# Another order of the seven products of an LSTM gate, other additions, and other places for the work beside them

## The chip, the cores and the metric

One core of a Trainium2 chip runs the whole program: TensorE (matrix products), VectorE, ScalarE and GpSimd (additions, activations), SyncE (which here issues transfers). The metric is the time on the device, in microseconds (us), from the first to the last instruction of one execution. Nothing is computed on the host except the layout of the inputs.

## What is computed

The reference is a stack of four residual layers on x (128 batches, 64 tokens, 256 channels) in float32; each is `x = x + layer(relu(layernorm(x)))`. Layers 0, 2 and 3 (a graph network with batch norm, and two kinds of attention) are not touched by the change. Layer 1 is:

```python
h = relu(einsum('ts,bsh->bth', adj, x @ Wg0 + bg0))      # "convolution"
h = relu(einsum('ts,bsh->bth', adj, h @ Wg1 + bg1))
for p in range(1, MAX_SKIP + 1):                         # p = 1, 2, 3, 4
    nw = T // p                                          # windows of p tokens
    wins = h[:, :nw * p, :].reshape(B * nw, p, H)
    last = lstm_last(Wih[p-1], Whh[p-1], bih[p-1], bhh[p-1], wins)
    h = h.at[:, arange(nw) * p + (p - 1), :].set(last)   # the last token of each window
# one LSTM step; gates i, f, g, o
g = x_t @ Wih.T + h @ Whh.T + bias
c = sigmoid(f) * c + sigmoid(i) * tanh(gg)
h = sigmoid(o) * tanh(c)
```

## The kernel before

The tokens go through layer 1 in eight superchunks of 1,024. A superchunk runs the LSTMs of p = 1 (`single`), 2, 3 and 4 (`lstm`) one after the other, each with p steps. Beside them, at the places where the generator of the LSTMs yields, stand pieces of other work: the two convolutions of the next superchunk (`convolutions`), the residual sums of the last one, and the start of layer 2 (`ahead`).

A 256 x 256 product of a gate is made of seven 128 x 128 products instead of eight, with sums of operands made beforehand (`operands_x` on GpSimd for x, `differences` on VectorE for h). A `Unit` is one gate at one step. Each of its products has an x part and an h part, added up by TensorE in a PSUM bank. Products 1, 6, 7 and 4 of a unit use one "x" bank one after the other, so each must be read before the next is written; product 5 uses a "y" bank, 2 and 3 the halves of a "z" bank. There are two banks of each letter.

```python
class Unit:                                   # cut
        self.of = {1: "x", 6: "x", 7: "x", 4: "x", 5: "y", 2: "z", 3: "z"}
    def copy(self, kind):                     # ScalarE: product 1 or 5 out of its bank
        nc.scalar.copy(gate(self.q, kind // 5, halves[kind // 5]), self.psum(kind))
    def add(self, dst, a, kind):              # VectorE: gate = gate + bank
        nc.vector.tensor_add(gate(self.q, *dst), gate(self.q, *a), self.psum(kind))
    def c11(self): self.add((0, halves[0]), (0, halves[0]), 2)
    def u4(self):  self.add((0, halves[1]), (1, halves[1]), 6)    # reads product 5's copy
    def c12(self): self.add((0, halves[1]), (0, halves[1]), 3)
    def c22(self): self.add((1, halves[1]), (1, halves[1]), 7)
    def act(self, part): ...                  # ScalarE; act(2) reads product 4 in the bank

for s in range(1, p):                         # one step; pe(k) = product k, do(f) = other engines
    last = s == p - 1
    B = [Unit(q, s) for q in (1, 3)]          # A: gates 0 and 2 (i, g); B: gates 1 and 3 (f, o)
    ...
    each(A, pe(5, "h"), do("copy", 5), pe(1), do("copy", 1), pe(3, "h"), pe(6, "x"), pe(6, "h"),
         pe(2, "h"), do("u4"), do("c11"), do("c12"))
    each(B, pe(5), do("copy", 5))
    each(A, do("act", 0), pe(7), do("c22"), do("act", 1))
    each(B[:1], pe(3), pe(2))
    each(A, pe(4), do("act", 2))
    nc.gpsimd.tensor_mul(gates[:, 0, :, :n], gates[:, 0, :, :n], gates[:, 2, :, :n])
    each(B[1:], pe(3), pe(2))
    each(B, pe(1), do("copy", 1))
    yield                                     # the middle of a step: an even place
    each(B, pe(6))
    A = [] if last else [Unit(q, s + 1) for q in (0, 2)]
    each(A, pe(5, "x"))
    def cell(c, part): ...                    # two VectorE operations, then tanh on ScalarE
    if last:
        ...                                   # see the diff
    else:
        for u in B:
            each([u], do("u4"), do("c11"), do("c12"), do("act", 0))
        cell(0, every)
        each(B, pe(7), do("c22"))
    each(B, do("act", 1))
    each(A[:1], pe(3, "x"), pe(2, "x"))
    new_state(s, 0, every)                    # VectorE; h for the next step, channels 0 to 127
    if not last: dh[0]()
    each(A[1:], pe(3, "x"), pe(2, "x"))
    each(B, pe(4))
    B[0].act(2); cell(1, halves[1]); B[1].act(2); cell(1, halves[0])
    new_state(s, 1, halves[1]); ...; new_state(s, 1, halves[0]); ...; dh[2]()
    yield                                     # the end of a step: an odd place
```

`each(us, f, g)` does f for every unit of `us`, then g. The places of a superchunk are numbered: 0 to 3 lie in `single`; 4, 8 and 14 between the first and the second half of the first products of p = 2, 3 and 4; 5, 9 and 15 ahead of their first step; then an even number for the middle and an odd one for the end of each step (6, 7; 10 to 13; 16 to 21). `CONV`, `BEGUN`, `FIRST` (the first superchunk) and so on say at which place each piece of the other work is put.

The engines' instructions stand in the order in which the program names them[...].

Of the kernel before, what the change touches and what calls it, by code (L numbers as in the profile page):

```python
# [19 lines left out]
def kernel(  # L20
# [23 lines left out]
    B, T, D = x.shape  # L44
# [12 lines left out]
    SUP = 2  # L57
# [531 lines left out]
    with tc.manual_schedule(engines={mybir.EngineType.PE, mybir.EngineType.DVE,  # L589
# [27 lines left out]
        for c in range(2, NCH - 1):  # L617
            a, z = sevens[c], sevens.get(c - 1)
# [273 lines left out]
    hTs = {}  # L892
# [87 lines left out]
    def convolutions(c):  # L980

        y, h = conv_tile(c)
        for m in range(KD):
            scaled(y, c, m)

        mid = res.tile([P, Q, CH * KD // Q], F32, tag=f"r{c}", name=f"ym_{c}")
        for k in range(KD):
            nc.vector.transpose(
                mid.rearrange("p b (j k c) -> p k j b c", j=NJ, k=KD)[:, k],
                y[:, k, :].rearrange("p (j b t) -> p j b t", b=Q, t=32))  # L990
        far = put(mid, f"y{c}")
        dst = y.rearrange("p k (q n) -> p (k q) n", q=2)
        get(dst, far)
        xs[c] = res.tile([P, NJ, D], F32, tag=f"r{c}", name=f"xs_{c}")
        nc.sync.dma_start(xs[c], xr[c])
        yield
        add_squares(xs[c], xs[c], dst)
        yield
        stats = ln_stats(xs[c], f"b{c}")
        yield  # L1000
        yield from apply_halves(h, xs[c], stats, f"b{c}")
        banks = aggregate(h, adjt_bd, f"b{c}")
        yield
        for e, ps in enumerate(banks):
            nc.vector.tensor_copy(by_batch(y)[:, e], ps)
        yield
        banks = product_v(c, y)
        yield
        bounded(y, banks)
        yield  # L1010
        banks = product_u(c, y)
        yield
        biased(h, banks)
        yield
        banks = aggregate(h, adjt_bd, f"c{c}")
        yield
        for e, ps in enumerate(banks):
            to_hT(c, e, ps)
            yield
# [30 lines left out]
    def lstm(p, hv, name, follows, x1, ending):  # L1050
# [3 lines left out]
        n = nb * nw  # L1054
# [85 lines left out]
        class Unit:  # L1140
# [25 lines left out]
            def c11(self):  # L1166
                self.add((0, halves[0]), (0, halves[0]), 2)

            def u4(self):
                self.add((0, halves[1]), (1, halves[1]), 6)  # L1170

            def c12(self):
                self.add((0, halves[1]), (0, halves[1]), 3)

            def c22(self):
                self.add((1, halves[1]), (1, halves[1]), 7)
# [9 lines left out]
        def each(us, *fs):  # L1186
            for f in fs:
                for u in us:
                    f(u)

        def pe(kind, parts="xh"):
            return lambda u: u.product(kind, parts)

        def do(f, *a):
            return lambda u: getattr(u, f)(*a)
# [4 lines left out]
        for s in range(1, p):  # L1200
            last = s == p - 1
            B = [Unit(q, s) for q in (1, 3)]
            if not last:
                ox[s + 1] = operands_x(p, hv, name, s + 1)
            each(A, pe(5, "h"), do("copy", 5), pe(1), do("copy", 1), pe(3, "h"), pe(6, "x"), pe(6, "h"),
                 pe(2, "h"), do("u4"), do("c11"), do("c12"))
            each(B, pe(5), do("copy", 5))
            each(A, do("act", 0), pe(7), do("c22"), do("act", 1))
            each(B[:1], pe(3), pe(2))
            each(A, pe(4), do("act", 2))  # L1210
            if last:
                load_sets(2)
            nc.gpsimd.tensor_mul(gates[:, 0, :, :n], gates[:, 0, :, :n], gates[:, 2, :, :n])  # L1213
            each(B[1:], pe(3), pe(2))
            each(B, pe(1), do("copy", 1))
            yield
            each(B, pe(6))
            A = [] if last else [Unit(q, s + 1) for q in (0, 2)]
            each(A, pe(5, "x"))

            def cell(c, part):
                nc.vector.tensor_mul(cells[:, c, part], cells[:, c, part], gate(1, c, part))
                nc.vector.tensor_add(cells[:, c, part], cells[:, c, part], gate(0, c, part))  # L1223
                nc.scalar.activation(gate(2, c, part), cells[:, c, part], AF.Tanh)  # L1224

            if last:

                each(B[:1], do("u4"), do("c11"), pe(7))
                each(B[1:], do("u4"), pe(7))
                each(B[:1], do("c22"), do("c12"), do("act", 0))  # L1230
                each(B[1:], do("c22"), do("c11"), do("c12"), do("act", 0))
                cell(0, every)
            else:
                for u in B:
                    each([u], do("u4"), do("c11"), do("c12"), do("act", 0))
                cell(0, every)
                each(B, pe(7), do("c22"))
            each(B, do("act", 1))
            each(A[:1], pe(3, "x"), pe(2, "x"))
            new_state(s, 0, every)  # L1240
            if not last:
                dh[0]()
            each(A[1:], pe(3, "x"), pe(2, "x"))
            each(B, pe(4))
            B[0].act(2)
            cell(1, halves[1])
            B[1].act(2)
            cell(1, halves[0])
            new_state(s, 1, halves[1])
            if not last:  # L1250
                dh[1]()
            new_state(s, 1, halves[0], nc.gpsimd if follows and last else nc.vector)
            if last:
                load_sets(2)
                ending()
            else:
                dh[2]()
            yield
# [212 lines left out]

    RESIDUAL = (0, 3, 4), (2, 5, 6)
    CONV = (3, 4, 4, 5, 6, 7, 8, 9, 10, 10), (3, 4, 4, 11, 12, 13, 14, 15, 16, 17, 18, 20)
    BEGUN = (11, 13, 14, 16), (17, 19)
    BEGUN_FIRST = (12, 15, 16, 18), (19, 21)
    FIRST = (1, 3, 3, 4, 4, 5, 6, 7, 8, 9, 10, 11, 12, 12), (3, 6, 7, 8, 10, 13, 14, 15, 16, 17, 18, 19, 20, 20)
    AHEAD = (4, 5, 7, 12, 14, 15), (6, 7)
    LATE = 5, 6, 8, 9  # L1480
    IDLE = {5: 4, 7: 18, 9: 10, 13: 14, 15: 8}
    FINAL = (4, 5, 10, 12, 12, 14), (6, 7, 11, 14, 14, 16)
    START = (0, 1, 0, 0, 0, 1, 0, 1, 1, 0, 0, 1, 1, 0, 1)

    tc.no_sync_barrier()
    with tc.manual_schedule(engines={mybir.EngineType.PE, mybir.EngineType.DVE, mybir.EngineType.Pool,
# [21 lines left out]
    with tc.manual_schedule(engines={mybir.EngineType.PE, mybir.EngineType.DVE, mybir.EngineType.Pool,  # L1508
                                     mybir.EngineType.Activation, mybir.EngineType.SP}):
        last = NCH // SUP - 1  # L1510
        for sc in range(last + 1):
            todo = {}

            def units(places, unit):
                for n in places:
                    todo.setdefault(n, []).append(unit)
# [17 lines left out]
                    units((FINAL if sc == last else AHEAD)[i], aheads[(sc - 1) * SUP + i])  # L1534
            if sc + 1 < last:
                for i in range(SUP):
                    units((BEGUN if sc else BEGUN_FIRST)[i], convs[(sc + 2) * SUP + i])
            for n, _ in enumerate(lstms(sc, hTs[sc])):
                for u in todo.pop(n, ()):
                    next(u)  # L1540
                if sc == last and n in IDLE:
                    keep_busy(IDLE[n], f"l{n}")
                if sc == last and n == 8:

                    new_hT(sc + 1)
                    for c in range(SUP):
                        load2(c, hTs[sc + 1][:, c, :].rearrange("p (q n) -> p q n", q=Q))
# [530 lines left out]
```

## Time and profile before

| | |
|---|---|
| device time, median of 3 runs | 1891.58 us (1890.7 to 1891.86) |
| span of the profiled execution | 1890.8 us |
| TensorE matmul, weight load, busy share | 99%, 78% |
| VectorE, ScalarE, GpSimd, busy share | 65%, 54%, 29% |
| first superchunk of layer 1 (274.2 to 437.1 us) | 162.9 us |
| each of the next five, which are alike | 155.6 us |
| seventh | 155.9 us |
| eighth, to its last LSTM product | 145.5 us |

The ends of matmuls are modelled in this profile, so "busy" holds short waits too; starts are recorded, and the distance from one start to the next shows them. Each float32 product of the program is two instructions of TensorE in the trace. In groups, "x<-xd" says which tile is written and which is read: x, y, z are the banks above, xd and hd the sums of operands of x and of h, hs and hT the states and the tokens themselves.

### The profile page before, as it was taken

How to read it: one execution, taken by the hardware profiler on the slowest of the kernel's cores; microseconds unless marked ns; L12 is line 12 of the kernel's file. 1: busy time of each engine (PE TensorE's matmuls, PEld its weight loads, DVE VectorE, ACT ScalarE, POOL GpSimd, SP SyncE). 2: the span in 40 equal slices, each digit the busy share in tenths (PEclk: the TensorE clock that was granted, in tenths of full speed). 3: DMA queues.
4: the chain of work that ended last, by engine and by line, in shares of the span. 5: the costliest groups of instructions: out<-in, count | busy, mean ns of one | idle time of the engine just before them, and what ended most of it. 6: DMA issues, size and time to landing. Idle time of an engine off the chain costs nothing.

```text
span 1890.8 us, 39088 instructions
## 1 busy us (share of the span) xinstructions
PE 1863.0 (99%) x15077; PEld 1479.3 (78%) x15077; DVE 1236.6 (65%) x3150; ACT 1016.6 (54%) x2284; POOL 551.4 (29%) x704
## 2 busy tenths in 40 slices
PE   8999989999999999999999999999999999999998
PEld 6877856886897798699589689878969967777776
DVE  6768845567476666667667666665565567676776
ACT  5766544456456446555655645655565544444453
POOL 5856622122222212212322321222122114332232
PEclk9999999999999999999999999999999999999999
DMA  3224643135333433332433343343144254444433
GB/s 114 73 66 150 234 175 105 49 116 184 106 129 139 151 129 129 110 124 114 151 118 139 141 151 129 129 135 117 52 135 154 71 157 135 143 148 142 139 113 113
DMA packets 111273, 241.45 MB, mean 128 GB/s; under 512 B 11504, under 2 KB 74864, under 8 KB 111088
## 3 DMA queue, kind: packets, MB, share of 16 engines
q1 hardware_dynamic: 110192, 237.09, 37.4%
q8 instruction: 119, 1.95, 0.4%
q0 software_dynamic: 320, 1.05, 0.2%
q10 hardware_dynamic: 576, 0.82, 0.1%
q14 instruction: 66, 0.54, 0.1%
HBM read 170.50 MB, written 68.42 MB: 126 GB/s over the span
## 4 chain that ended last, share of the span: by engine, by line
PE 90%; DVE 5%; ACT 2%; issue 1%; POOL 1%; DMA 1%; SPq 0%; DVEq 0%; ACTq 0%
PE x L1155 23%; PE z L1155 11%; PE g L1126 9%; PE y L1155 6%; PE v L1568 6%; PE x L1329 4%; PE y L1329 3%; PE u L929 3%; PE p_q L1575 3%; PE v L915 3%; PE X L1764 3%; PE X L423 2%; PE X L499 2%; PE Y L1764 1%; PE Y L423 1%
## 5 line engine op out<-in xcount | busy, mean ns | idle before, releaser
L1164 DVE TENSOR_TENSOR gates<-gates,x 128x128 f32<-128x128 f32 (+2 forms) x384 | 118.5, 321 | 326.3 <-PE x L1155 319.1
L1155 PE MATMUL x<-xd,wset 128*128 128x128 f32 (+2 forms) x1152 | 256.8, 311 | 0.7 <-DVE gates L1164 0.2
L1155 PE MATMUL x<-hd,wset 128*128 128x128 f32 (+2 forms) x1152 | 246.7, 303 | 0.0
L1213 POOL TENSOR_TENSOR gates<-gates 128x512 f32<-128x512 f32 (+2 forms) x48 | 75.0, 1562 | 551.8 <-ACT gates L1084 551.8
L1084 ACT ACTIVATE gates<-gates,bias 128x256 f32<-128x256 f32 (+4 forms) x384 | 170.3, 490 | 56.2 <-DVE gates L1164 52.7
L1155 PEld LDWEIGHTS x<-xd,wset 128*128 128x128 f32 x1152 | 180.8, 190 | 19.0 <-DVE gates L1164 6.1
L1155 PEld LDWEIGHTS x<-hd,wset 128*128 128x128 f32 x1152 | 185.1, 191 | 5.0
L1126 PE MATMUL g<-hT,wset 128*128 128x256 f32 (+2 forms) x576 | 183.9, 474 | 1.1 <-DVE hT L1095 1.1
L1126 PEld LDWEIGHTS g<-hT,wset 128*128 128x128 f32 x576 | 108.6, 190 | 69.8 <-issue 38.5
L1161 ACT COPY gates<-y 128x128 f32<-128x128 f32 (+2 forms) x192 | 54.3, 294 | 202.3 <-PE y L1155 201.8
L1155 PE MATMUL z<-hs,wset 128*128 128x128 f32 (+2 forms) x768 | 154.0, 303 | 0.0
L1155 PE MATMUL z<-hT,wset 128*128 128x128 f32 (+2 forms) x768 | 148.4, 306 | 0.0
L1155 PEld LDWEIGHTS z<-hs,wset 128*128 128x128 f32 x768 | 119.8, 191 | 3.3
L1155 PEld LDWEIGHTS z<-hT,wset 128*128 128x128 f32 x768 | 117.9, 192 | 4.4 <-ACT gates L1113 0.5
L1161 ACT COPY gates<-x 128x128 f32<-128x128 f32 (+2 forms) x192 | 56.6, 296 | 93.5 <-PE x L1155 92.8
L1164 DVE TENSOR_TENSOR gates<-gates,z 128x128 f32<-128x128 f32 (+2 forms) x384 | 104.5, 316 | 0.1
L1084 ACT ACTIVATE gates<-x,bias 128x128 f32<-128x128 f32 (+2 forms) x192 | 74.8, 390 | 49.3 <-PE x L1155 46.5
L1113 ACT ACTIVATE gates<-g,bias 128x512 f32<-128x512 f32 (+2 forms) x144 | 74.6, 560 | 30.7 <-PE g L1126 30.2
L1155 PE MATMUL x<-hT,wset 128*128 128x128 f32 (+2 forms) x384 | 85.7, 305 | 0.4 <-ACT gates L1084 0.2
L1155 PE MATMUL x<-hs,wset 128*128 128x128 f32 (+2 forms) x384 | 84.9, 303 | 0.0
L1224 ACT ACTIVATE gates<-cell 128x256 f32<-128x256 f32 (+2 forms) x144 | 55.3, 384 | 51.9 <-DVE cell L1223 50.3
L1155 PE MATMUL y<-xd,wset 128*128 128x128 f32 (+2 forms) x384 | 77.4, 304 | 3.9 <-ACT gates L1113 3.3
(326 smaller groups left out, 4144.6 us busy)
## 6 DMA issues: line engine op xcount, KB each, us to landing
wset<-wfar SPq DMA_DIRECT2D x96, 960.0 KB, 6.5
hT<-far_h SPq DMA_DIRECT2D x124, 128.0 KB, 3.1
far_h<-hm SPq DMA_DIRECT2D x16, 512.0 KB, 2.8
far_n<-xs SPq DMA_DIRECT2D x16, 512.0 KB, 3.5
xs<-far_n SPq DMA_DIRECT2D x64, 128.0 KB, 3.7
far_x<-xs SPq DMA_DIRECT2D x16, 512.0 KB, 3.0
x<-far_x SPq DMA_DIRECT2D x64, 128.0 KB, 3.2
xt<-in_x_dram SPq DMA_DIRECT2D x15, 512.0 KB, 4.1
```

The source lines that it names most:

```text
L423: nc.tensor.matmul(self.banks[tag][:, i * CH // 2 : (i + 1) * CH // 2], w, self.at[kind], start=first and not i, stop=True, skip_group_che ...
L915: nc.tensor.matmul(banks[m], wg0_sb[:, k, m * P : (m + 1) * P], agg[:, k, :], start=(k == 0), stop=(k == KD - 1))
L1084: nc.scalar.activation(gate(q, c, part), src, AF.Tanh if q == 2 else AF.Sigmoid, bias=bs[:, q * KD + c : q * KD + c + 1])
L1113: nc.scalar.activation(columns_of(gate(q, c)), natural(banks[q, c][:, :n].rearrange("p (w b) -> p w b", b=nb)), AF.Tanh if q == 2 else AF. ...
L1126: nc.tensor.matmul(banks[q, c][:, :n].rearrange("p (w b) -> p w b", b=nb), wsets[p, q][:, 2 * k + c, :], hv[:, k, : (nw - 1) * p + 1 : p, ...
L1155: nc.tensor.matmul(folded(self.psum(kind)), wsets[p, self.q][:, BLOCKS[kind][i], :], (ox[self.s] if part == "x" else oh)[kind], start=firs ...
L1161: nc.scalar.copy(gate(self.q, kind // 5, halves[kind // 5]), self.psum(kind))
L1164: nc.vector.tensor_add(gate(self.q, *dst), gate(self.q, *a), self.psum(kind))
L1213: nc.gpsimd.tensor_mul(gates[:, 0, :, :n], gates[:, 0, :, :n], gates[:, 2, :, :n])
L1329: nc.tensor.matmul(folded(ps(g, kind)), wih1[:, g, KINDS1[kind], :], right[kind], start=kind in (2, 5, 1), stop=True, skip_group_check=True)
L1568: nc.tensor.matmul(ps[:, i, :], hT[:, k, j, :], w[:, k, first : first + D], start=(k == 0), stop=(k == KD - 1))
L1764: nc.tensor.matmul(st[c, tag][:, i * CH // 2 : (i + 1) * CH // 2].rearrange("p (a n) -> p a n", n=P), w, st[c, "o7"][kind], start=first an ...
```

## The change

Products and additions are put in another order, so that between two writes of the same x bank other products stand; in the units that have room for it, product 3 is added first (`v5`) and product 6 after it (`u5`), so that fewer additions wait for product 6. A new half place ("a", number 5.5, 9.5, and so on) ahead of the B units takes pieces of VectorE work that stood at the middle of a step. `convolutions` gets one more yield, so that its first piece (`scaled`) and its transposes can stand at two places; and the first superchunk gets the places that the others have, for which the first convolution of the second superchunk begins before layer 1's LSTMs (two more entries of `START`).

```diff
@@ convolutions
         for m in range(KD):
             scaled(y, c, m)
-
+        yield
         mid = res.tile(...)                      # two transposes on VectorE follow
@@ Unit
+            def v5(self):
+                self.add((0, halves[1]), (1, halves[1]), 3)
+            def u5(self):
+                self.add((0, halves[1]), (0, halves[1]), 6)
@@ the step
-            each(A, pe(5, "h"), do("copy", 5), pe(1), do("copy", 1), pe(3, "h"), pe(6, "x"), pe(6, "h"),
-                 pe(2, "h"), do("u4"), do("c11"), do("c12"))
-            each(B, pe(5), do("copy", 5))
-            each(A, do("act", 0), pe(7), do("c22"), do("act", 1))
-            each(B[:1], pe(3), pe(2))
-            each(A, pe(4), do("act", 2))
+            each(A, pe(5, "h"), do("copy", 5), pe(1), do("copy", 1), pe(3, "h"), pe(2, "h"), pe(6), do("u4"),
+                 do("c11"), do("c12"))
+            each(B[:1], pe(5), do("copy", 5))
+            each(A, pe(7), do("c22"), do("act", 0))
+            each(B[1:], pe(5), do("copy", 5))
+            each(A, pe(4), do("act", 2), do("act", 1))
+            yield "a"
+            each(B[:1], pe(3))
             if last:
                 load_sets(2)
             nc.gpsimd.tensor_mul(gates[:, 0, :, :n], gates[:, 0, :, :n], gates[:, 2, :, :n])
-            each(B[1:], pe(3), pe(2))
             each(B, pe(1), do("copy", 1))
+            each(B[:1], pe(2), do("v5"), do("c11"))
+            if not last:
+                each(B[1:], pe(3), pe(2), do("v5"), do("c11"))
             yield
             each(B, pe(6))
+            if last:
+                each(B[1:], pe(3))
             A = [] if last else [Unit(q, s + 1) for q in (0, 2)]
             each(A, pe(5, "x"))
@@ after the definition of cell
+            each(B[:1], do("u5"), do("act", 0))
             if last:
-                each(B[:1], do("u4"), do("c11"), pe(7))
-                each(B[1:], do("u4"), pe(7))
-                each(B[:1], do("c22"), do("c12"), do("act", 0))
-                each(B[1:], do("c22"), do("c11"), do("c12"), do("act", 0))
+                each(B[1:], do("u4"))
+                each(B, pe(7), do("c22"))
+                each(B[1:], pe(2), do("c11"), do("c12"), do("act", 0))
                 cell(0, every)
             else:
-                for u in B:
-                    each([u], do("u4"), do("c11"), do("c12"), do("act", 0))
+                each(B[1:], do("u5"), do("act", 0))
+                each(B, pe(7))
                 cell(0, every)
-                each(B, pe(7), do("c22"))
+                each(B, do("c22"))
@@ places
-    RESIDUAL = (0, 3, 4), (2, 5, 6)
-    CONV = (3, 4, 4, 5, 6, 7, 8, 9, 10, 10), (3, 4, 4, 11, 12, 13, 14, 15, 16, 17, 18, 20)
-    BEGUN = (11, 13, 14, 16), (17, 19)
-    BEGUN_FIRST = (12, 15, 16, 18), (19, 21)
-    FIRST = (1, 3, 3, 4, 4, 5, 6, 7, 8, 9, 10, 11, 12, 12), (3, 6, 7, 8, 10, 13, 14, 15, 16, 17, 18, 19, 20, 20)
+    RESIDUAL = (0, 3, 4), (2, 5, 5.5)
+    CONV = (3, 4, 4, 5, 5.5, 7, 8, 9, 10, 10), (3, 4, 4, 11, 11.5, 13, 14, 15, 15.5, 17, 18, 20)
+    BEGUN = (11, 11, 13, 14, 16), (17, 17.5, 19)
+    FIRST = (1, 2, 3, 3, 4, 4, 5, 5.5, 7, 8, 9, 10, 10), (3, 3, 5.5, 7, 8, 8, 11, 11.5, 13, 14, 15, 15.5, 17, 18, 20)
-    START = (0, 1, 0, 0, 0, 1, 0, 1, 1, 0, 0, 1, 1, 0, 1)
+    START = (0, 1, 0, 0, 0, 1, 0, 1, 1, 0, 0, 1, 1, 0, 1, 2, 2)
@@ the loop over superchunks
-                    units((BEGUN if sc else BEGUN_FIRST)[i], convs[(sc + 2) * SUP + i])
-            for n, _ in enumerate(lstms(sc, hTs[sc])):
+                    units(BEGUN[i], convs[(sc + 2) * SUP + i])
+            n = -1
+            for mark in lstms(sc, hTs[sc]):
+                n = n + 0.5 if mark else int(n) + 1
```

## The prediction, made before the changed kernel ran

> **What bounds the kernel now.** I read the page's busy times and its chain first:
>
> ```profile
> PE 1863.0 (99%) x15077; PEld 1479.3 (78%) x15077; DVE 1236.6 (65%) x3150; ACT 1016.6 (54%) x2284; POOL 551.4 (29%) x704
> ...
> PE 90%; DVE 5%; ACT 2%; issue 1%; POOL 1%; DMA 1%; SPq 0%; DVEq 0%; ACTq 0%
> ```
>
> TensorE bounds the kernel, and the change removes no product. All it can win is time in which TensorE stands still between products, and 99% seems to leave none. But ends are modelled, so I went to starts. In the timeline of TensorE at p = 4, step 2 (fifth superchunk), columns start, length, group:
>
> ```profile
> 1042.30 0.39 PE L1155 MATMUL x<-hT,wset 128*128 128x128 f32 x2
> 1042.52 0.39 PE L1155 MATMUL x<-hs,wset 128*128 128x128 f32 x2
> 1042.81 0.49 PE L1155 MATMUL x<-xd,wset 128*128 128x128 f32 x2
> 1043.14 0.39 PE L1155 MATMUL x<-hd,wset 128*128 128x128 f32 x2
> 1043.36 0.39 PE L1155 MATMUL x<-xd,wset 128*128 128x128 f32 x2
> ```
>
> Pairs normally start 0.224 us apart, 0.112 an instruction. From 1042.52 to 1042.81 it is 0.29, and from 1042.81 to 1043.14 0.33: 0.07 of waiting and then 0.10 more. The group at 1042.81 is product 6 of B1, which waits for ScalarE's copy of product 1 out of the same x bank. So a wait costs TensorE its length plus about 0.10 us, and the page counts next to none of it as idle. The same view of all engines 5 us earlier:
>
> ```profile
> 1035.61 1.00 DVE L900 TENSOR_SCALAR cv<-z1a,sc_bn,sh_bn 128x512 f32<-128x512 f32 x2
> ...
> 1036.64 1.30 DVE L988 STREAM_TRANSPOSE ym<-cv 128x512 f32<-128x512 f32 x2
> ...
> 1037.73 0.39 PE L1155 MATMUL y<-hd,wset 128*128 128x128 f32 x2
> 1037.87 0.45 DVE L1164 TENSOR_TENSOR gates<-gates,x 128x128 f32<-128x128 f32 x2
> ...
> 1038.17 0.30 PEld L1155 LDWEIGHTS x<-xd,wset 128*128 128x128 f32 x2 [0.25 <-DVE gates L1164]
> ```
>
> Here two scalings and two transposes of a convolution hold VectorE until 1037.87, and product 7 of A0 waits for the addition of product 6.
>
> I subtracted the usual distance (0.112, 0.143, 0.216, 0.429 us for 128, 168, 256, 512 columns) from every distance of starts in the trace, leaving out 64-column products, and added up what exceeds 0.02. Layer 1 holds about 37 us: 9.8 in the first superchunk, 3.5 in each of the next five, 3.8 in the seventh, 5.7 in the eighth. In the fifth, by the product that waited: product 6 of B 0.69 (five steps), product 4 of B 0.83 (five), product 7 of B in last steps 0.45, product 7 of A 0.32, the start of p = 4 step 3 (product 5, and product 1 of A2) 0.34; the other 0.8 is mostly the change to and from the 64-column products of the convolutions.
>
> The first superchunk differs most:
>
> ```profile
> 297.47 7.03 PE L1126 MATMUL g<-hT,wset 128*128 128x512 f32 x16
> 307.00 1.18 PE L1155 MATMUL y<-xd,wset 128*128 128x256 f32 x4 [2.51 <-ACT gates L1113]
> 308.06 3.59 PE L1155 MATMUL z<-hT,wset 128*128 128x256 f32 x8
> ```
>
> ```profile
> 304.21 2.07 ACT L196 ACTIVATE cv<-xs,nmr_b,rstd_b 128x256 f32<-128x256 f32 x4 [7.10 <-DVE nmr_b L194]
> 306.19 2.39 ACT L1113 ACTIVATE gates<-g,bias 128x512 f32<-128x512 f32 x4
> ```
>
> Four normalizations of the next convolution (L196) stand on ScalarE before the first activations of p = 2, and wait 7.1 us for statistics that VectorE makes late. The first y and z products stand still about 4.3 us over their usual distances.
>
> [...]
>
> **The change part by part.** I measure a step in product parts: 0.224, 0.286 and 0.432 us at p = 4, 3, 2. An addition issues every 0.20 us at p = 4, and takes about 0.28, with 0.2 from the end of a product part to its use.
>
> B, 1 before 6. Before, two parts (0.45) stood between product 1 of B1 and its 6; copy 0.27 plus hand-overs 0.3 did not fit. Now product 2 of B1 and, in a step that isn't the last, 3 and 2 of B3 stand there also: 4 or 8 parts. The 0.69 goes.
>
> B, 6, 7, 4. Before, six additions followed product 6, and the cell's two operations and `c22` came behind. Now four are made before the middle and two `u5` are left. At p = 4, `c22` of B1 ends about 2.7 us after the middle, and product 4 stands 14 parts (3.1) after it; before, 3.1 against 3.1. In last steps 3 and 2 of B3 put two more parts before product 7 and two before 4. The 0.83 and 0.45 go.
>
> A. 6 now comes after 2, so from 6 to 7 of A0 there are four parts (0.9) where there were seven. The addition is ready about 3.2 us after the step's start, product 7 stands at 3.6: it fits if VectorE is free by 2.9. In the case shown the transposes move to place 17.5, and it is free at 1.6. The 0.32 goes. Product 4 then has c22 at 4.6 against 4.9: it fits, with little room.
>
> The start of p = 4 step 3. VectorE comes about 0.6 earlier, so product 1 of A2 (0.34 with product 5) nearly fits. But product 2 of A moves from the twelfth to the eighth part, 1.8 us into the step, and needs the state that I place at 1.7 to 1.75. I leave 0.2 of waiting here.
>
> So an ordinary superchunk loses 0.69 + 0.83 + 0.45 + 0.32 + 0.34 - 0.2 = 2.4 us; I count 2.2 for what I have placed too well. Six of them: 13.
>
> First superchunk. Squares now stand at place 1, statistics at 2, normalizations at 3, in place of 3, 3 and 4: VectorE has 1.6 us free at 294.1 for them. The aggregation's products at place 4 give 1.3 us more. I expect about 0.5 of the 4.3 to stay. Its B waits (1.8 in all) go too. At p = 3 there is 1.1 of the same kind; both normalizations stand at place 8 now instead of one, so that this may grow by 0.3. Place 19 no longer has products to cover the step 3 start: 0.2. In `single` the wait at 291.4 (0.46) may halve. Together -3.8 - 1.8 + 0.3 + 0.2 - 0.2 = -5.3; I take 5. The two pieces moved into the start stage cost VectorE 2.3 us between 274.1 and 279.6, where it is idle: nothing.
>
> Eighth superchunk. It has the same B waits, 1.7 us, the p = 4 starts of 0.8 to 1.3, of which I count half, and 0.4 at the start of p = 3. But its list of places is unchanged, with statistics (2.1 us of VectorE) at the middle 10 and four transposes (1.3) at the middle 16. In the old program nothing stood on VectorE between the A additions and the middle, so these ran early; now `v5` and `c11` of both B stand before them, and they run when `u5` is wanted. I make that +1.1 and +0.8. Net -0.7.
>
> Sum: -13 - 5 - 0.7 = -18.7; predicted 1873.5 us (1891.6 less 18), 0.95% faster.
>
> **The rivals.** First: the waits change place. A's distances are cut (6 to 7, 7 to 4, 4 to B1's 1)[...]; if its additions run 0.3 us later than I have them, product 7 or 4 of A waits in each of the six steps, at 0.15 to 0.25 each: 0.9 to 1.5 a superchunk, and the time is 1880 to 1885. For it: the margins of 0.3. Against: the additions' distance of 0.20 is read from this trace, and p = 2 and 3 have longer parts. Second: the waits are hidden anyway, as VectorE or ScalarE sets the pace and a removed wait returns one product later. Then only the first superchunk gains: 1886. Against: VectorE is 65% busy in these windows, and idle 3.97 us ahead of the middle at 1043.6. Third: all fits, product 2 of A too, and the first superchunk comes down to 155.6: -16, -7, -2, or 1866.
>
> **Range and chances.** Working from the trace's starts bounds the gain: all of layer 1's stand-still is 37 us, under 2% (37.8 us), and part of it is the cost of changing product shapes. Faster by over 2% is as good as excluded. Slower by over 2% needs 38 us more, or 0.8 us in each of 48 steps; no margin is missed by so much. Eight in ten: 1866 to 1882.
>
> **What would show it.** In the changed trace: ordinary superchunks of about 153.3 us; no stand-still at product 6 of B; products 7 and 4 of B at usual distance; L196's four normalizations before 302 and no wait at the first y products of p = 2; in the eighth, statistics behind the B additions and product 7 of B waiting at p = 3 step 1. Superchunks at 154.5 or more, with waits at products 7 or 4 of A, prove the first rival; waits at product 2 of A of more than 0.3 prove my states too early. A first superchunk above 160 makes the places' part wrong.

## The result, and the profile after

| | before | after |
|---|---|---|
| device time, median | 1891.14 us (1890.46 to 1891.86) | 1877.2 us (1876.15 to 1879.19) |
| ratio | | 0.9927, 95% interval 0.9910 to 0.9945 |
| span of the profiled execution | 1890.8 us | 1877.4 us |
| first superchunk | 162.9 us | 158.2 us |
| second to sixth | 155.6 us each | 153.9, 154.9, 154.8, 153.7, 157.2 us |
| seventh | 155.9 us | 153.0 us |
| eighth, to its last LSTM product | 145.5 us | 146.3 us |
| after layer 1's last LSTM product | 374.5 us | 371.5 us |

The kernel became 0.7% faster. 1877.2 lies in the predicted range (1866 to 1882), 3.7 us above the predicted 1873.5. But the parts don't agree as well as the sum: layer 1 gave 10 us of the 18.7 worked out for it, and 3 us came from behind layer 1, where nothing was predicted.

The page of the changed kernel, busy times and chain:

```profile
PE 1847.4 (98%) x15077; PEld 1476.8 (79%) x15077; DVE 1245.6 (66%) x3150; ACT 1014.0 (54%) x2284; POOL 550.2 (29%) x704
...
PE 86%; DVE 6%; DMA 2%; ACT 2%; issue 1%; POOL 1%; SPq 0%; DVEq 0%; ACTq 0%
```

The instruction counts are those of before. TensorE's busy time fell by 15.6 us with the same products: "busy" held the short waits, as the prediction took it. DMA's share of the chain grew from 1% to 2%: a transfer has come into it.

Busy times by stretch of the changed kernel: one line each for the first superchunk, the second, the sixth, the seventh, the eighth and what follows. The columns are start and end, length, busy time of TensorE, its weight loads, VectorE, ScalarE and GpSimd (instructions in brackets), granted clock of TensorE, DMA share, GB/s:

```profile
273.90:432.10 158.20, 156.10 (x1155) 127.11 (x1156) 97.03 (x257) 84.39 (x203) 34.24 (x41) 1.00 0.29 102
432.10:586.00 153.90, 153.45 (x1092) 125.80 (x1091) 99.67 (x269) 84.52 (x208) 34.91 (x42) 1.00 0.37 129
1049.50:1206.70 157.20, 155.13 (x1093) 127.48 (x1092) 103.31 (x282) 86.58 (x212) 36.19 (x44) 0.99 0.38 130
1206.70:1359.60 152.90, 152.90 (x1092) 125.63 (x1091) 93.87 (x261) 85.68 (x210) 33.48 (x42) 1.00 0.33 112
1359.60:1505.90 146.30, 142.99 (x841) 118.72 (x840) 86.61 (x253) 82.53 (x203) 33.74 (x42) 1.00 0.37 116
1505.90:1877.40 371.50, 364.33 (x4323) 272.29 (x4322) 261.45 (x555) 164.80 (x306) 106.03 (x129) 1.00 0.46 139
```

The second and the sixth superchunk hold the same work and differ by 3.3 us, where before five superchunks agreed within 0.03. The seventh has the same 1092 or 1093 instructions of TensorE and is the shortest; it is also the only one of the first seven that has no next-but-one superchunk's convolution (the list `BEGUN`) beside it. So what went wrong in the ordinary superchunks is in the pieces of `BEGUN`.

Almost all the waits that the change aimed at are gone. TensorE at p = 4, step 2, fifth superchunk, the place shown of before:

```profile
1033.87 0.39 PE L1155 MATMUL x<-xd,wset 128*128 128x128 f32 x2
1034.09 0.39 PE L1155 MATMUL x<-hd,wset 128*128 128x128 f32 x2
1034.32 0.39 PE L1155 MATMUL x<-xd,wset 128*128 128x128 f32 x2
```

Product 6 of B1 and of B3 follow each other at 0.22 and 0.23: no 0.29, no 0.33. I added up the distances of starts as in the prediction. Over 0.02 us there is now no wait at product 6 of B in any superchunk, none at product 7 of B in last steps, none at product 7 of A in step 2 of p = 4, and none at product 4 of B outside p = 4 step 1 but for 0.08 us in the eighth superchunk. The stand-still of layer 1 went from 37.0 us to 27.2.

The first superchunk, TensorE and ScalarE around the start of p = 2:

```profile
297.81 2.08 ACT L196 ACTIVATE cv<-xs,nmr_b,rstd_b 128x256 f32<-128x256 f32 x4 [1.59 <-DVE nmr_b L194]
...
300.33 5.42 PE L1126 MATMUL g<-hT,wset 128*128 128x512 f32 x12
...
301.55 1.49 ACT L1113 ACTIVATE gates<-g,bias 128x512 f32<-128x512 f32 x2 [1.67 <-PE g L1126]
...
305.58 1.03 PE L1155 MATMUL y<-xd,wset 128*128 128x256 f32 x4
```

The four normalizations wait 1.6 us instead of 7.1 and are done at 299.9; the activations begin 4.6 us sooner in the run; the first y products follow the g products without a wait. The 4.3 us there are gone to the last tenth.

What is new appears in the same sum of distances: a wait at product 7 of A0 in p = 4 step 3, of 0.96, 0.48, 1.44, 1.33, 0.28 and 2.10 us in the first six superchunks; 0.50 us at product 4 of B1 in p = 4 step 1, the same in all six; 1.57 and 1.01 us at product 7 of B1 in the eighth, and there also 0.37 at product 7 of A0 in p = 3 step 2 and 0.41 at product 2 of A0 in p = 4 step 2. The largest, in the sixth superchunk, timeline of VectorE, TensorE and SyncE's queue:

```profile
1183.99 1.30 DVE L988 STREAM_TRANSPOSE ym<-cv 128x512 f32<-128x512 f32 x2
...
1185.32 0.32 SPq L247 DMA_DIRECT2D far_y<-ym  x1
...
1189.89 1.74 SPq L254 DMA_DIRECT2D cv<-far_y  x4
...
1191.68 0.43 SPq L995 DMA_DIRECT2D xs<-in_x_dram  x1
...
1193.43 0.29 DVE L316 TENSOR_TENSOR hd<-hs,hd 128x128 f32<-128x128 f32 x1
...
1195.11 0.39 PE L1155 MATMUL y<-hd,wset 128*128 128x128 f32 x2
...
1195.79 1.29 DVE L284 TENSOR_TENSOR xs<-xs,cv 128x512 f32<-128x512 f32 x2 [2.06 <-DMA xs<-in_x_dram]
...
1197.33 0.49 PE L1155 MATMUL x<-xd,wset 128*128 128x128 f32 x2 [1.84 <-DVE gates L1164]
```

A convolution's tile goes from the transposes to memory (L247) and comes back (L254), and the tile it is added to is fetched behind it on the same queue (L995); then VectorE adds the two and the squares follow (L284, in `BEGUN` the 19). VectorE reaches L284 at 1193.7. The fetch has not landed. VectorE stands for 2.06 us, with the LSTM's additions behind L284, and product 7 of A0 waits for one of these. In all six superchunks VectorE reaches L284 8.4 us after the put is issued; the operands are there 9.3, 8.8, 9.8, 9.7, 8.6 and 10.5 us after it, and the differences are the waits, 0.9, 0.4, 1.4, 1.3, 0.2 and 2.1. In the kernel before, VectorE reached L284 in the sixth superchunk 11.5 us after the put, with no wait:

```profile
1193.53 0.32 SPq L247 DMA_DIRECT2D far_y<-ym  x1
...
1205.02 1.29 DVE L284 TENSOR_TENSOR xs<-xs,cv 128x512 f32<-128x512 f32 x2
```

The 0.50 at product 4 of B1, fifth superchunk, the same engines with ScalarE:

```profile
1019.78 0.49 DVE L1164 TENSOR_TENSOR gates<-gates,z 128x128 f32<-128x128 f32 x2 [0.34 <-PE z L1155]
...
1020.18 0.15 DVE L194 SCALAR_TENSOR_TENSOR nmr_b<-mv_b,rstd_b 128x4 f32<-128x4 f32 x1
...
1020.37 1.09 ACT L196 ACTIVATE cv<-xs,nmr_b,rstd_b 128x256 f32<-128x256 f32 x2 [1.67 <-DVE nmr_b L194]
...
1021.37 0.89 ACT L1084 ACTIVATE gates<-gates,bias 128x256 f32<-128x256 f32 x2
...
1021.89 0.42 DVE L1234 TENSOR_TENSOR cell<-cell,gates 128x256 f32<-128x256 f32 x1 [0.94 <-ACT gates L1084]
```

`nmr_b` (0.15 us, place 16) stands behind `v5` and `c11` on VectorE, which wait for products 3 and 2. So ScalarE's two normalizations begin at 1020.37, and B's sigmoid behind them a microsecond later; the cell's first operation waits 0.94 for it, then comes `c22`, then product 4.

And the eighth at p = 3 step 1, VectorE and TensorE:

```profile
1435.83 0.42 DVE L159 BATCH_NORM_STATS2 st_n<-xs 128x6 f32<-128x256 f32 x1
...
1437.86 0.18 DVE L160 BATCH_NORM_AGGREGATE mv_n<-st_n 128x2 f32<-128x6 f32 x1
1437.96 0.53 DVE L1164 TENSOR_TENSOR gates<-gates,x 128x168 f32<-128x168 f32 x2
...
1438.31 0.55 PE L1155 MATMUL x<-xd,wset 128*128 128x168 f32 x2 [1.30 <-DVE gates L1164]
```

Statistics for 2.1 us hold the two `u5`, as predicted.

Behind layer 1, TensorE's waits from 1500 us on, before and after (columns: what waits, for what, us in total, times, longest):

```profile
PE s L1843 <- issue: 2.3, 2, 1.2
PE p_q L1575 <- PE s L1843: 1.0, 1, 1.0
```

```profile
PE s L1855 <- issue: 0.5, 1, 0.5
```

The lines of code are the same (L1843 is L1855 in the changed kernel). 2.8 of the 3.0 us that were gained there are these. "Issue" means that the profile shows nothing waited for.

### The profile page after: what moved, and what is told of

It reads as the page before. It is cut to its first block, busy times and chain, and to the rows that moved or that the text cites. A ratio compares the mean times of both kernels' runs of the same rounds, so it can differ in the third digit from the quotient of the medians.

```text
span 1877.4 us, 39077 instructions
## 1 busy us (share of the span) xinstructions
PE 1847.4 (98%) x15077; PEld 1476.8 (79%) x15077; DVE 1245.6 (66%) x3150; ACT 1014.0 (54%) x2284; POOL 550.2 (29%) x704
## 4 chain that ended last, share of the span: by engine, by line
PE 86%; DVE 6%; DMA 2%; ACT 2%; issue 1%; POOL 1%; SPq 0%; DVEq 0%; ACTq 0%
PE x L1155 20%; PE z L1155 10%; PE g L1126 9%; PE v L1580 5%; PE y L1155 5%; PE x L1340 4%; PE y L1340 3%; PE v L915 3%; PE u L929 3%; PE p_q L1587 3%; PE X L1776 3%; PE X L423 2%; PE X L499 2%; PE Y L1776 1%; PE Y L423 1%
## 5 line engine op out<-in xcount | busy, mean ns | idle before, releaser
L1155 PE MATMUL x<-hd,wset 128*128 128x128 f32 (+2 forms) x1152 | 255.3, 303 | 0.0
L1155 PEld LDWEIGHTS x<-xd,wset 128*128 128x128 f32 x1152 | 188.2, 192 | 16.6 <-DVE gates L1164 11.6
L1155 PE MATMUL z<-hs,wset 128*128 128x128 f32 (+2 forms) x768 | 146.5, 303 | 0.2 <-DVE hs L1093 0.2
L1155 PE MATMUL y<-hd,wset 128*128 128x128 f32 (+2 forms) x384 | 79.7, 310 | 0.0
```

The costliest lines, as they stand in the source:

```text
L1155: nc.tensor.matmul(folded(self.psum(kind)), wsets[p, self.q][:, BLOCKS[kind][i], :], (ox[self.s] if part == "x" else oh)[kind], start=firs ...
```

## The experiments

The theory after the result has three parts. T1: the waits at product 7 of A0 come from L284, which is reached before its transfer lands, as the transposes went back by half a step and L284 stayed. T2: the 0.50 comes from `nmr_b` behind `v5` and `c11`. T3: the order by itself is worth little or less than nothing; it pays when the pieces on VectorE are moved ahead of the additions that it put in front of the middle. The rival, R, is the prediction's own first one: the waits have changed place because A's shorter distances (6 to 7, 7 to 4) leave VectorE too little time, and transfers only show it.

**One place for the squares.** The number 19 becomes 19.5, half a step later.

```diff
-    BEGUN = (11, 11, 13, 14, 16), (17, 17.5, 19)
+    BEGUN = (11, 11, 13, 14, 16), (17, 17.5, 19.5)
```

> The changed kernel with one place changed: the squares of the second convolution (VectorE, they need the transposed tile read back from memory) stand at 19.5 instead of 19. Theory, late landing: with the transposes at 17.5 the tile lands after VectorE reaches place 19, and [...]the addition of product 6 and so product 7 of A wait behind the squares at p = 4 step 3. Then the wait of product 7 there (0.28 to 2.1 us in the first six superchunks, 6.6 in the trace's sum, and about 1.3 more of lowered clock after the longest) is gone: about 1870 us. Rival, tight A: product 7 waits because only four product parts stand between 6 and 7 and VectorE comes late by itself; then the wait stays at 0.2 to 0.5 in each and the time is 1875 or more.

Measured: 1871.12 us (1870.22 to 1871.31), ratio to before 0.9894 (0.9877 to 0.9910). The second to the sixth superchunk take 153.45 or 153.46 us, all five. The sixth, the same engines:

```profile
1180.45 0.32 SPq L247 DMA_DIRECT2D far_y<-ym  x1
...
1186.73 0.43 SPq L995 DMA_DIRECT2D xs<-in_x_dram  x1
...
1190.24 0.39 PE L1155 MATMUL y<-hd,wset 128*128 128x128 f32 x2
...
1190.47 0.39 PE L1155 MATMUL x<-xd,wset 128*128 128x128 f32 x2
...
1191.84 1.29 DVE L284 TENSOR_TENSOR xs<-xs,cv 128x512 f32<-128x512 f32 x2
```

L284 comes 11.4 us after the put and waits for nothing, and product 7 of A0 (1190.47) stands at the usual 0.23 behind product 5 of B1. A's order was not touched. So the distance from 6 to 7 of A does hold, and R is refuted as the cause of these waits; T1 stands.

**One place for the norm's `nmr_b`.** The 16 becomes 15.5, ahead of the B units.

```diff
-    BEGUN = (11, 11, 13, 14, 16), (17, 17.5, 19)
+    BEGUN = (11, 11, 13, 14, 15.5), (17, 17.5, 19)
```

> The changed kernel with one place changed: the first two normalizations of the first convolution (a small VectorE operation, nmr, then two on ScalarE) stand at 15.5 instead of 16. Theory: at 16 nmr stands on VectorE behind v5 and c11 of both B, so ScalarE makes the normalizations only after the middle, the sigmoid of B comes behind them, the cell and c22 too, and product 4 of B at p = 4 step 1 waits 0.50 us in six superchunks. At 15.5 all six go: about 3.0 us less, 1874. Rival: the chain from product 6 over sigmoid, cell and c22 is too long by itself at that step; the 0.5 stays and the time is 1877.

Measured: 1874.64 us (1873.47 to 1875.8), ratio 0.9912 (0.9897 to 0.9927). All six waits of 0.50 are gone, and the waits at product 7 of A0 stay (0.85, 0.50, 1.12, 1.45, 0.32, 2.16). The median is 2.6 us below the changed kernel's: six times 0.5 are 3.0. T2 stands.

**The transposes back.** The other way to give the round trip time: the transposes at 17, where they stood behind the scalings in the kernel before.

```diff
-    BEGUN = (11, 11, 13, 14, 16), (17, 17.5, 19)
+    BEGUN = (11, 11, 13, 14, 16), (17, 17, 19)
```

> The changed kernel with the second convolution's transposes back at 17, beside the scalings, and the squares at 19. Late landing expects that the tile is back in time (some 5 us earlier): product 7 of A at p = 4 step 3 doesn't wait, but the two transposes hold VectorE at the start of step 2, where product 7 of A then waits 0.3 to 0.6: about 1872. Tight A expects the wait at step 3 to stay and that at step 2 to be added: 1879 or more.

Measured: 1876.23 us (1875.34 to 1877.0), ratio 0.9921 (0.9906 to 0.9935). The waits in step 3 fall to 0.05 or 0.06, as T1 has it. In their place stands 0.77 in step 2 of every one of the six, more than the 0.3 to 0.6 expected: 1.0 to 2.8 us in six, of the some 4 us by which the time is above the 1872 expected. The fifth superchunk, VectorE and TensorE:

```profile
1026.18 1.00 DVE L900 TENSOR_SCALAR cv<-z1a,sc_bn,sh_bn 128x512 f32<-128x512 f32 x2
...
1027.21 1.31 DVE L988 STREAM_TRANSPOSE ym<-cv 128x512 f32<-128x512 f32 x2
...
1028.44 0.45 DVE L1164 TENSOR_TENSOR gates<-gates,x 128x128 f32<-128x128 f32 x2
...
1028.75 0.49 PE L1155 MATMUL x<-xd,wset 128*128 128x128 f32 x2 [0.51 <-DVE gates L1164]
```

2.3 us of VectorE at the start of the step hold the addition of product 6, as they did before, where product 7 then stood three product parts later: 0.32 there, 0.77 here. This is what the splitting of the transposes into a place of their own was for, and why `convolutions` got its yield. The transposes may stand at 17.5 or the squares at 19, not both.

**The order alone.** All places as before (with the old `FIRST`, `START` and no added yield in `convolutions`), the products and additions in the new order.

```diff
-    RESIDUAL = (0, 3, 4), (2, 5, 5.5)
-    CONV = (3, 4, 4, 5, 5.5, 7, 8, 9, 10, 10), (3, 4, 4, 11, 11.5, 13, 14, 15, 15.5, 17, 18, 20)
-    BEGUN = (11, 11, 13, 14, 16), (17, 17.5, 19)
+    RESIDUAL = (0, 3, 4), (2, 5, 6)
+    CONV = (3, 4, 4, 5, 6, 7, 8, 9, 10, 10), (3, 4, 4, 11, 12, 13, 14, 15, 16, 17, 18, 20)
+    BEGUN = (11, 13, 14, 16), (17, 19)
```

> The new order of products and additions with all places of the kernel before (no half places, first superchunk on its own places, transposes beside the scalings). Theory, order and places belong together: the waits of products 6 and 4 of B go (some 2 us a superchunk), but the VectorE pieces at the middles 6, 12 and 16 now stand behind v5 and c11 and hold u5, so that product 7 of B waits in three steps, 2 us a superchunk in all; first superchunk unchanged at about 162: 1887 to 1891. Rival, the order does it alone: 2.2 us less in each of seven superchunks and nothing in the first: 1876.

Measured: 1908.34 us (1905.89 to 1908.8), ratio 1.0088 (1.0073 to 1.0103): slower than the kernel before, and 17 us more than the most that was expected. Ordinary superchunks take 157.6 to 157.8. Product 7 of B1 waits 1.3 to 1.4 at p = 2, 0.8 at p = 3 step 2 and 0.97 at p = 4 step 1, with 0.73 at product 4 behind it; and product 7 of A0 waits 0.77 at p = 4 step 2, behind the transposes, which stand at 17 again. The first superchunk takes 170.4. Its largest wait, at p = 4 step 1, VectorE and TensorE:

```profile
406.31 0.48 DVE L1164 TENSOR_TENSOR gates<-gates,z 128x128 f32<-128x128 f32 x2 [0.34 <-PE z L1155]
...
406.71 1.28 DVE L921 TENSOR_TENSOR cv<-v,nc 128x512 f32<-128x512 f32 x2
...
407.91 0.41 DVE L159 BATCH_NORM_STATS2 st_b<-xs 128x6 f32<-128x256 f32 x1
...
410.04 0.45 DVE L1164 TENSOR_TENSOR gates<-gates,x 128x128 f32<-128x128 f32 x2
410.35 0.80 PE L1155 MATMUL x<-xd,wset 128*128 128x128 f32 x2 [2.74 <-DVE gates L1164]
```

The pieces at a middle place are named behind `v5` and `c11` of B3 (406.31). VectorE stands idle for 2.91 us before those of B1 (405.49) and for 0.34 before 406.31 and starts none of the pieces in that time; it starts them at 406.71, when product 2 of B is done, and `u5` (410.04) stands behind 3.3 us of them. T3 stands, and more strongly than I had it: the half place "a" isn't an addition to the order, the order needs it.

**The first superchunk's places alone**, on the kernel before.

```diff
-    FIRST = (1, 3, 3, 4, 4, 5, 6, 7, 8, 9, 10, 11, 12, 12), (3, 6, 7, 8, 10, 13, 14, 15, 16, 17, 18, 19, 20, 20)
+    FIRST = (1, 2, 3, 3, 4, 4, 5, 6, 7, 8, 9, 10, 10), (3, 6, 7, 8, 8, 11, 12, 13, 14, 15, 16, 17, 18, 20)
```

Also `START` gets one more 2, and the first superchunk uses `BEGUN`.

> The kernel before with the first superchunk's new places alone (half places moved up to the next middle, one piece of the first convolution in the start stage, the second superchunk's convolutions begun at the common places); order of products as before. Theory: the places alone take away the 4.3 us of waiting at the first y and z products of p = 2, and leave some 1.3 at p = 3; the first superchunk takes 158 to 159.5 us in place of 162.9, the others 155.6, and the time is 1887 to 1888. Rival, the places help only with the new order: 1890 or more.

Measured: 1888.67 us (1887.76 to 1889.63), ratio 0.9985 (0.9978 to 0.9991). The first superchunk takes 159.7 us, 3.2 less, against 158 to 159.5 expected. The stand-still of the first four products of p = 3 grew from 1.1 to 2.1 (1.7 in the changed kernel). The other superchunks stay at 155.6. So of the first superchunk's 4.7 us some 3 are the places' and the rest the order's.

**The half order, twice.** First the A units with products 6 before 2 and both products 5 of B ahead of 7, the rest changed:

```diff
-            each(A, ..., pe(3, "h"), pe(2, "h"), pe(6), do("u4"), do("c11"), do("c12"))
-            each(B[:1], pe(5), do("copy", 5))
-            each(A, pe(7), do("c22"), do("act", 0))
-            each(B[1:], pe(5), do("copy", 5))
-            each(A, pe(4), do("act", 2), do("act", 1))
+            each(A, ..., pe(3, "h"), pe(6), pe(2, "h"), do("u4"), do("c11"), do("c12"))
+            each(B, pe(5), do("copy", 5))
+            each(A, do("act", 0), pe(7), do("c22"), do("act", 1))
+            each(A, pe(4), do("act", 2))
```

> The changed kernel with gates i and g (A) in their old product order (6 ahead of 2, both 5 of B between 6 and 7, nothing of B between 7 and 4), B and all places as changed. Theory: for A the new order trades room between 6 and 7 for room between 7 and 4; with the old one here product 7 of A at p = 4 step 3 waits about 0.45 less in six superchunks (2.7 us in all), but product 4 of A stands two parts after 7 of A2 and waits 0.2 to 0.3 for c22 in each p = 4 step, 5 to 6 us in all: 1879 to 1881. Rival, the new A order only costs: 1874.5.

Measured: 1885.69 us (1884.78 to 1886.67), ratio 0.9970 (0.9959 to 0.9981); more than the 1879 to 1881 expected. Product 4 of A0 now waits in every step of p = 3 (0.18, twice) and p = 4 (0.26, 0.26, 0.35): 1.23 a superchunk. Those at p = 3 I had not expected. This isn't quite the old A, where products 3 and 2 of B1 stood between 7 and 4; these belong to B's new order, and without them nothing is left between 7 and 4. The product 5 of B3 that the change puts there is what keeps product 4 from waiting. The shorter waits that I expected at product 7 of A0 in p = 4 step 3 did not come either: 0.44, 0.15, 1.20, 1.15, 0.86 and 2.44 us, 6.2 in all against 6.6, though eight product parts now stand between products 6 and 7 where the change has four. That speaks against R once more.

Then the B units with the old order of products and additions, A and all places changed:

```diff
-            each(B[:1], pe(3))
+            each(B[:1], pe(3), pe(2))
             nc.gpsimd.tensor_mul(...)
+            each(B[1:], pe(3), pe(2))
             each(B, pe(1), do("copy", 1))
-            each(B[:1], pe(2), do("v5"), do("c11"))
-            if not last:
-                each(B[1:], pe(3), pe(2), do("v5"), do("c11"))
             yield
```

and the additions after `cell` and the product 3 of B3 in last steps as in the kernel before.

> The changed kernel with gates f and o (B) in their old order of products and additions; A and all places as changed. Theory: the waits of B return (product 6 0.69, product 4 0.83, product 7 in last steps 0.45 a superchunk), those at middle places go as VectorE has nothing of B ahead of the middle (product 4's 0.50 in six superchunks, product 7's 2.6 in the eighth), and product 7 of A at p = 4 step 3 waits as long or longer for the late tile: 1884 to 1889. Rival, A's order and the places make the gain, and B's gives little: 1878 to 1880.

Measured: 1888.6 us (1886.64 to 1890.1), ratio 0.9985 (0.9979 to 0.9992). The waits at product 6 of B (0.085 at p = 3, 0.17 at p = 4), at 4 and at 7 come back; the 0.50 at product 4 and the eighth's 1.57 and 1.01 are gone, for no `v5` or `c11` stands ahead of the middle's pieces. The late squares cost up to 1.36 here too. So the gain needs B's order, without which 2.9 us of it are left; the same order made two of the three new kinds of wait. It needs A's too: with half of that taken back, 8.5 us were lost.

**All places put right.** The squares at 19.5, `nmr_b` at 15.5, and in the eighth superchunk the statistics at 9.5 and the last transposes at 15.5, all ahead of the B units:

```diff
-    BEGUN = (11, 11, 13, 14, 16), (17, 17.5, 19)
+    BEGUN = (11, 11, 13, 14, 15.5), (17, 17.5, 19.5)
-    FINAL = (4, 5, 10, 12, 12, 14), (6, 7, 11, 14, 14, 16)
+    FINAL = (4, 5, 9.5, 12, 12, 14), (6, 7, 11, 14, 14, 15.5)
```

> The changed kernel with the squares at 19.5, the first normalizations at 15.5, and in the eighth superchunk statistics at 9.5 in place of 10 and four transposes at 15.5 in place of 16. Theory, VectorE pieces at a middle hold u5 and product 7 of B: the squares bring 6 us and the normalizations 3, as measured one at a time, and product 7 of B no longer waits 1.57 and 1.01 us in the eighth: 1865 to 1866. Rival, the eighth superchunk's waits come from its missing convolutions, not from these places: 1868.

Measured: 1864.41 us (1864.01 to 1864.88), ratio 0.9858 (0.9842 to 0.9874). Ordinary superchunks take 152.95 us, the eighth 143.2; its waits of 1.57 and 1.01 are gone. The three causes nearly add up: 6.1 us for the squares and 2.6 for `nmr_b`, as measured one at a time, and 3.1 in the eighth superchunk are 11.8 of the 12.8 us between the changed kernel and this one.

**More places.** The starts of p = 3 in the first superchunk and of p = 4 in the eighth: `FIRST` has 9, 9 for 8, 8, and `FINAL` moves the pieces of the second list by half a step to a step and a half. The diff is against the changed kernel; `BEGUN` is as in the run before.

```diff
-    FINAL = (4, 5, 10, 12, 12, 14), (6, 7, 11, 14, 14, 16)
+    FINAL = (4, 5, 9.5, 12, 12, 14), (6, 7, 11.5, 15, 15, 17.5)
```

> As the one before, and three more places: in the first superchunk the second convolution's normalizations at 9 in place of 8, so that they don't stand on ScalarE ahead of the first activations of p = 3 (1.35 + 0.36 us of waiting); in the eighth statistics at 11.5 for 11, both normalizations at 15 for 14 (1.0 + 0.35 us at the start of p = 4), and the last transposes at 17.5. Expected: 1.5 us less from the first and 1.5 to 2 from the eighth, 1862 to 1863. If ScalarE's and VectorE's queues only shift the waits, it stays at 1865.

Measured: 1863.24 us (1862.53 to 1863.5), ratio 0.9852 (0.9837 to 0.9866). First superchunk 155.4, eighth 142.8: there two new waits, 1.12 at product 6 of A0 in p = 4 step 1 and 0.38 at product 7 of B1, take back part of it. A last step spreads the same pieces (`FIRST` 9, 9.5; `FINAL` 6, 7, 13, 15, 15.5, 17.5).

> The changed kernel with squares at 19.5, first normalizations at 15.5, the second convolution's normalizations of the first superchunk at 9 and 9.5, and in the eighth superchunk statistics at 9.5 and 13, normalizations at 15 and 15.5, transposes at 17.5. Against the version before it (more places, 1863.2): product 6 of A no longer waits 0.32 in the first and 1.1 in the eighth superchunk behind four normalizations on ScalarE, and product 7 of B not 0.38 in the eighth: 1861.5 to 1862. If the waits only move on, 1863.

Measured: 1862.11 us (1861.95 to 1862.67), ratio 0.9842 (0.9828 to 0.9855). Busy times by stretch of this kernel, first, second and eighth superchunk:

```profile
274.40:429.40 155.00, 154.94 (x1154) 126.98 (x1155) 97.72 (x257) 84.20 (x203) 34.27 (x41) 1.00 0.29 103
429.40:582.40 153.00, 153.00 (x1093) 125.74 (x1093) 100.37 (x269) 84.62 (x208) 34.80 (x42) 1.00 0.38 130
1347.30:1489.70 142.40, 141.47 (x842) 118.51 (x841) 87.92 (x253) 82.72 (x203) 34.44 (x42) 1.00 0.38 119
```

It beats both kernels: 29 us less than before, twice what the change gave, with the same instruction counts as before on the four compute engines. Of the 1.12 at product 6 of A0 in the eighth, 0.8 is still there. The stand-still of layer 1 is 10.5 us by the same sum, of which some 0.8 a superchunk is the change to and from 64-column products.

## Why the prediction was right, and where it was not

**B, 1 before 6** and **B, 6, 7, 4**: right in every step but one in the first seven superchunks. "The 0.69 goes" and "the 0.83 and 0.45 go": 0.69 and 0.45 went, and of the 0.83 a wait of 0.50 came back in one step. The sentence that failed is "now four are made before the middle and two `u5` are left". It counts additions only. I had the same thing written down for the eighth superchunk ("now `v5` and `c11` of both B stand before them, and they run when `u5` is wanted") and didn't ask which pieces stand at a middle in the ordinary ones. `nmr_b` at 16 does. It is 0.15 us of VectorE, but a microsecond of ScalarE follows from it: 6 × 0.50 = 3.0 us, shown by moving it.

**A.** The working of the distances was right: no product 4 of A waits, and the 0.32 in step 2 went. What failed is "in the case shown the transposes move to place 17.5, and it is free at 1.6. The 0.32 goes", as an end of the matter. A piece that was moved back has a consumer. The put takes 4.4 us in the sixth superchunk and the fetch behind it 4.0, and with what lies between, the squares' operands are there 8.6 to 10.5 us after the put, where VectorE now comes after 8.4. Before, it came after 11.5, and the fetch had landed 2.3 us earlier (1202.74); the move took away 3.1. The sum of the waits is 6.6 us, and 1.5 more of a lowered clock (0.50 for 3.4 us) follow the longest (below). The slack that the move used up stood in the trace of the kernel before, in the start of the put and of L284, and I read neither.

**First superchunk.** "I take 5", and 4.7 came, with 1.5 us of the new waits inside it, so that the old ones gave 6.2. Of the 4.3 nothing stayed where I left 0.5. But only 2.8 of it had been standing still: the rest was a lowered clock behind the wait (0.54 granted from 308.5 to 312.0, last section), which I took for more waiting, as both lengthen the distances of starts. "This may grow by 0.3" at p = 3: 1.1 became 1.7. In `single` the wait of 0.46 went.

**Eighth.** Net -0.7 predicted, +0.9 measured. Place and cause were right, the sizes short: 1.57 for 1.1 and 1.01 for 0.8, together 0.7 too little. The start of p = 4, which I counted as half gone, stands still 1.5 us (0.98 at its first product). And 0.37 at product 7 of A0 in p = 3 step 2, where statistics hold its addition, was not counted at all.

**The sum.** Without the new waits, the second to seventh superchunk would have given 15.7 us (155.56 less 152.95, six times) where I counted 13. So the ordinary superchunk's sum was too careful by 0.4 each, and the new waits took 12.7 in all: 6.6 + 1.5 + 3.0 in the first six, and 1.6 more than counted in the eighth. 18.7 + 2.7 (ordinary) + 1.2 (first) - 12.7 leaves 9.9; measured 10.

**The rivals.** The first had its sign in three of the five ordinary superchunks, 154.5 us or more with waits at product 7 of A, and that would have "proved" it. Its mechanism was not there: the place of the squares alone removed all of them and left A's distances as they were. A sign that two causes share proves neither. The second is refuted: no removed wait came back one product later. The third, "all fits", put -16, -7, -2 to the three parts. With the places right the parts are -15.7, -6.2 and -2.3, and the time 1864.4.

**The start of p = 4 step 3**: "I leave 0.2 of waiting here". It is 0.13, at product 1 of A2, and product 2 of A doesn't wait there. In step 2 of the eighth superchunk it does: 0.41 us, for VectorE's state, over the 0.3 that the prediction set as the sign of states placed too early. It is one step of the 48.

**Behind layer 1** nothing was predicted, and 3.0 us came. The stretch takes 374.5 us in the kernel before and 374.3 with the first superchunk's places alone; 372.1 with A's order, all new places and B's old order; 370.9 to 371.5 in every kernel with B's new order, on the old places too. So B's order is not needed for the larger part of it, nor are the new places; each figure is of one trace. Why waits without a shown cause, in code that is the same and some hundred microseconds later, should depend on the order, no run here shows; that stays open. That the time came within 3.7 us of the predicted one is luck in part: without these 3 us it would have been some 1880, still in the range, 7 above 1873.5.

## What to carry to other kernels

When work is put ahead of a point in an engine's stream, list every other piece that stands at that point: each of them moves behind it, and here a piece of 0.15 us cost 0.5. When a producer whose tile goes through memory is moved, measure from its put to its consumer in the old trace, and move the consumer with it. And an order and its places belong together: the order alone made this kernel 0.9% slower, with the places it was given 0.7% faster, with the right ones 1.6%.

## What the runs showed of the hardware

TensorE's clock fell after some of the waits. The changed kernel, busy times by stretch, with most of the wait of 2.1 us in the sixth superchunk, right behind it, and later (the third column from the right is the granted clock):

```profile
1192.00:1197.00 5.00, 3.50 (x31) 3.25 (x29) 2.77 (x10) 1.76 (x8) 0.00 (x0) 1.00 0.54 154
1197.00:1201.30 4.30, 3.97 (x21) 3.97 (x22) 1.75 (x9) 1.54 (x4) 0.00 (x0) 0.60 0.00 0
1201.30:1206.00 4.70, 4.70 (x44) 4.70 (x44) 1.58 (x7) 2.85 (x8) 1.27 (x1) 1.00 0.90 337
```

From 1197.9 to 1201.3, 3.4 us, eight product parts stand 0.43 apart instead of 0.224, 1.9 times as far; the granted clock from 1197.88 to 1201.29 is 0.50. The wait before it was 2.1 us long. With the order alone the clock fell during a wait, one of 2.9 us: it is 1.00 from 406.0 to 409.0 and 0.70 in the mean from 409.0 to 411.3, and product 7 of B1 starts at 410.35; at 0.50 from there on, the mean would be 0.79. And nearly the same wait did not always do it: with `nmr_b` moved, product 7 of A0 in the sixth superchunk waited 2.16 us, and the four microseconds behind it ran at a granted clock of 1.00:

```profile
1194.00:1198.00 4.00, 3.97 (x35) 3.97 (x36) 1.45 (x7) 2.71 (x9) 0.31 (x1) 1.00 0.20 52
```

The kernel before had such a stretch too, which the prediction overlooked. Behind the 2.5 us for which the first y product of p = 2 waited in the first superchunk, the same view of the kernel before has

```profile
308.50:312.00 3.50, 3.50 (x32) 2.36 (x34) 2.76 (x6) 2.38 (x5) 0.00 (x0) 0.54 1.00 240
```

and the z products stand 0.43 apart instead of 0.216; 1.5 of the 4.3 us there are this. Waits of 1.44 us in the third superchunk and 1.57 in the eighth of the changed kernel lowered nothing that shows: the granted clock of both superchunks is 1.00, where the sixth, with its 3.4 us at 0.50, has 0.99. So a wait of over 2 us in a busy stretch was followed by a slow stretch that cost some 1.5 us more in these two traces. Its length alone does not decide it: besides the 2.16 us with `nmr_b` moved, a wait of 2.4 us with half of the old A (1202.38 to 1204.72) had no such stretch behind it; the mean granted clock of that whole trace is 1.000, and 3.4 us at 0.50 would make it 0.999. What decides it stays open.
